# First-layer softmax sums: two more groups of a batch, and six of the first batch, added up by VectorE in place of TensorE

## The chip, the cores and the metric

The kernel runs on one core of a Trainium2 chip. The metric is the device time of one execution in microseconds (us). The engines are TensorE (PE; PEld is its weight load), VectorE (DVE), ScalarE (ACT), GpSimd (POOL) and SyncE (SP), which here only issues DMAs.

## The reference, cut to what matters

Two layers, each a group norm, an attention over 1024 tokens of 512 channels, a projection and a residual, for a batch of 8 images of 32 x 32. All is 32-bit float. The change is in the attention of the first layer (16 heads of 32 channels):

```python
attn = jnp.einsum('bhid,bhjd->bhij', q * SCALE, k)
attn = jax.nn.softmax(attn, axis=-1)
out = jnp.einsum('bhij,bhjd->bhid', attn, v)
```

The second layer has 4 heads of 128 channels and adds relative position logits to its scores. A softmax row's sum is over all 1024 keys j; the kernel keeps keys on partitions, so that a sum over keys is a sum across partitions.

## The kernel before, in words

**Tiling.** Channels or keys lie on the 128 partitions. `attention_0` works in 8 groups per batch: a group is 4 heads (index m, in the order 0, 2, 1, 3; `HB` is 4 heads of `D0` = 32 channels) and a half h of the queries (`NB` = 512). Each group has 8 blocks of 128 keys (`NT`), so a batch has 64 steps. A step's `front` makes the scores of 4 heads on TensorE (L886: 32-row weights, two halves of the keys) into one 4-bank PSUM tile `ps` with a single buffer, and ScalarE's exponential (L901) writes 128 x 2048 numbers into one of three slots of `e_room`. The step after it, `back` multiplies the values with them on TensorE (L912) into the PSUM bank `acc`, which also has one buffer, and VectorE adds the block onto the group's running sum (L924, 7 of 8 blocks), in place in the slot of the group's first block. The slot of an ended group's sums goes back into the turn, and the exponential of the third block of the next group writes it.

**Sums of a group, two ways.** At the first step after a group has ended, a helper divides by the row sums:
- `finish` (L930): TensorE multiplies the 4 running sums with ones (L934), 8 instructions (a 32-bit matmul is two), into the `acc` bank. `normalise` has ScalarE copy them (L764), VectorE transpose (L766), invert (`invert`, L781 and L784) and spread them by another transpose (L796), and GpSimd multiply the group's 128 x 512 output in `q` (L770).
- `sums_apart` (L865) with the class `Apart` (L807): for a list of groups, `take` (L818) has VectorE transpose each head's running sum in blocks of 32 x 32 (L826) and reduce it (L829) into a column of `few_0`. It does two heads in one step and two in the next (the second half only behind the last product add, `reader[0]`). After the last group of the list, `fold_up` (L837) has TensorE add the 32 remaining partials of all its groups at once (L841, 8 short instructions) into a `bank`, VectorE inverts them, and `quotient` (L852), one group a step, spreads (L796) and has GpSimd multiply (L857).

`apart_of(b)` (L138) gives the lists of batch b. Before, `APART` is one list (2, 3, 4); batch 0 has none, batch 1 has (2, 3), batch 7 has (3, 4). In batches 2 to 6 the list (2, 3, 4) is not folded in place: `sums_apart` puts it into `aside`, and it is folded, inverted and multiplied at the end of the second layer's attention, which runs in the middle of the batch.

**Rings of tiles.** Tiles of one tag share buffers in turn, and a new tenant waits until the last one has been read. `rec`, two buffers of 128 x 512, serves `normalise`, `take` and `quotient`. `columns`, two buffers of the same size, holds the column part of the second layer's position logits: `Seeds.load` (L1037) brings one tile per 8 steps of `attention_1` by a DMA on SP, and GpSimd adds it (L1064). `bank`, three PSUM banks, serves the products and the folding.

**What sets the order.** The projections are made in seven products of half size (`seven`, L506): x, y and z are banks, `a` and `b` (L520, L528) are VectorE adds that read a bank between two products into it, and `c12`, `c21` (L682, L685) finish a quarter. `side_by_side` (L1611) interleaves the 64 steps of `attention_0` of batch b with the rest of the work, by costs: the first layer's output projection of b-1 and the second layer's of b-2, the second layer's projections, its attention (cost 0: it runs in one piece, at about step 42 of 64), and the first layer's projections for b+1 (`before_0`). In batch 0 only the rest of its own projections and `before_0` of batch 1 stand beside it, together with the preparation of weights on GpSimd (`other_sums`, L182). `issue_after` keeps an instruction behind another of its engine; apart from that the framework orders each engine's instructions by itself.

In the trace, batch 0's attention runs from 58 to about 306 us, batch 1's from there to 726, and a batch of 2 to 6 takes 442.0 us from one point to the same in the next. The second layer's attention of batch 1 (beside batch 2's first layer) lies from 952 to 1061; groups 5, 6 and 7 of batch 2 end at about 1091, 1131 and 1168.

Of the kernel before, what the change touches and what calls it, by code (L numbers as in the profile page):

```python
# [9 lines left out]
F32 = mybir.dt.float32  # L10
# [7 lines left out]
P = 128  # L18
# [4 lines left out]

BLOCKS = 8

APART = [(2, 3, 4)]


@with_exitstack
def quick_path(  # L30
# [25 lines left out]
    B, IH, IW, C = x.shape  # L56
# [3 lines left out]
    NB = 512  # L60
# [9 lines left out]
    mem = ctx.enter_context(tc.tile_pool(name="mem", bufs=1))  # L70
# [18 lines left out]
    def wide_tile(name, shape=None):  # L89
        return wide[0][1].tile(shape or [P, NB // P, NB], F32, tag="ps", name=name, bufs=1)  # L90
# [47 lines left out]
    def apart_of(b):  # L138
        if b == 1:
            return [(2, 3)] + APART[1:]  # L140
        return [] if b == 0 else [(3, 4)] if b == B - 1 else APART

    n_checks = B * CC * NH + 2 * 4 + B - 2
    n_checks -= sum(len(some) - 1 for b in range(B) for some in apart_of(b))
    checks = consts.tile([P, n_checks], F32, tag="checks", name="checks")
    check_at = [0]
# [10 lines left out]
    class Matrix:  # L157
# [3 lines left out]
        def __init__(self, w, col0, name):  # L161
            self.name = name
            self.w = w.rearrange("(cc p) n -> p cc n", p=P)[:, :, col0 : col0 + NB]
# [60 lines left out]
    class Stream:  # L224
# [43 lines left out]
        def take(self, i):  # L268
            got = self.tiles.pop((self.at, i)) if self.plan[self.at][2] else self.tiles[self.at, i]
            return got  # L270
# [487 lines left out]
    def normalise(dst, acc_sums, name, engine=nc.gpsimd):  # L758

        su = mem.tile([P, NB], F32, tag="rec", name=f"su_{name}", bufs=2)
        nc.scalar.copy(su, acc_sums)  # L764
        turned = mem.tile([P, NB], F32, tag="rec", name=f"tu_{name}", bufs=2)
        nc.vector.transpose(turned, su)  # L766
        few, rec = [turned.rearrange("p (t c) -> p t c", c=32)[:, :, i] for i in range(2)]
        invert(rec, few, few)
        spread(su, rec)
        engine.tensor_tensor(dst, dst, su, op=ALU.mult)  # L770
# [36 lines left out]
    class Apart:  # L807


        def __init__(self, b, some):  # L810
            self.b, self.some = b, some
            self.groups = []
            self.width = len(some) * (NB // 32)

        def place(self, r):
# [2 lines left out]
        def take(self, m, h, esum, dst):  # L818
            at = len(self.groups)
            self.groups.append((m, h, dst))  # L820
            for r0 in range(0, HB, 2):
                turned = []
                for r in (r0, r0 + 1):
                    t = mem.tile([P, NB], F32, tag="rec", name=f"tu_0_{self.b}_{m}_{h}_{r}", bufs=2)
                    with tc.issue_after(reader[0].ins) if r0 else nullcontext():
                        nc.vector.transpose(t, esum[:, r, :])  # L826
                    turned.append(t)
                for r, t in zip((r0, r0 + 1), turned):
                    nc.vector.tensor_reduce(  # L829
                        few_0[:, r, at, :],  # L830
                        t.rearrange("p (t c) -> p t c", c=32),
                        axis=AX.X,
                        op=ALU.add,
                    )
                yield
# [23 lines left out]
    def attention_0(q, k, v, b, blocks=range(NT)):  # L859

        steps = [(m, h, j) for m in (0, 2, 1, 3) for h in range(NH) for j in blocks]
        state = {}
        aparts = {i: part for some in apart_of(b) for part in [Apart(b, some)] for i in some}

        def sums_apart(i, m, h, esum):  # L865
            part = aparts[i]
            together = i == 4 and b < B - 1
            if together:
                aside.append(part)
            yield from part.take(m, h, esum, q[m][:, h * NB : (h + 1) * NB])  # L870
            if together or i != part.some[-1]:
                return
            part.fold_up()
            for i in range(len(part.some)):
                yield
                part.quotient(i)

        def front(m, h, j):
            name = f"0_{b}_{m}_{h}_{j}"
            ps = wide_tile(f"ps_{name}")  # L880
            for i in range(2):

                some = slice(64 * i, 64 * i + 64)
                for r in range(HB):
                    rows = slice(r * D0, (r + 1) * D0)
                    nc.tensor.matmul(  # L886
                        ps[some, r, :],
                        k[m][rows, j * P + 64 * i : j * P + 64 * i + 64],
                        q[m][rows, h * NB : (h + 1) * NB],
                        start=True,  # L890
                        stop=True,
                    )
            at = turn.pop(0)
            if j == blocks[0]:

                turn.append(sum_at[0])
                sum_at[0] = at
            else:
                turn.append(at)
            e = e_room[:, at]  # L900
            exps[0] = nc.scalar.activation(e, ps, AF.Exp, scale=D0 ** -0.5)  # L901
            return e

        def back(m, h, j, e):
            name = f"0_{b}_{m}_{h}_{j}"
            if j == blocks[0]:
                state["acc"] = psum.tile([P, NB], F32, tag="acc", name=f"acc_{name}", bufs=1)
                state["first"] = e
            acc = state["acc"]
            for r in range(HB):  # L910
                c0 = (m * HB + r) * D0
                nc.tensor.matmul(  # L912
                    acc[r * D0 : (r + 1) * D0, :],
                    v[:, j, c0 : c0 + D0],
                    e[:, r, :],
                    start=(j == blocks[0]),
                    stop=(j == blocks[-1]),
                )
            if j == blocks[1]:
                state["esum"] = state["first"]  # L920
            if j != blocks[0]:

                with tc.issue_after(reader[0].ins) if beside_norm[0] else nullcontext():
                    summed[0] = nc.vector.tensor_add(state["esum"], state["esum"], e)  # L924
            if j != blocks[-1]:
                return
            nc.scalar.copy(q[m][:, h * NB : (h + 1) * NB], acc)
            state["ended"] = (m, h, state["esum"])

        def finish(m, h, esum):  # L930
            name = f"0_{b}_{m}_{h}"
            su = psum.tile([P, NB], F32, tag="acc", name=f"sums_{name}", bufs=1)
            for r in range(HB):
                nc.tensor.matmul(  # L934
                    su[r * D0 : (r + 1) * D0, :],
                    ones,
                    esum[:, r, :],
                    start=True,
                    stop=True,
                )  # L940
            normalise(q[m][:, h * NB : (h + 1) * NB], su, name)

        pending = None
        ended, ending = 0, []
        for at in steps:
            if "ended" in state:
                if ended in aparts:
                    ending.append(sums_apart(ended, *state.pop("ended")))
                else:
                    finish(*state.pop("ended"))  # L950
                ended += 1
            for part in ending:
                next(part, None)
            e = front(*at)
            if pending is not None:
                back(*pending)
            pending = (*at, e)
            yield 2
        for part in ending:
            run(part)  # L960
        back(*pending)
        yield 1
        finish(*state.pop("ended"))
# [643 lines left out]
    def run(part):  # L1607
        for _ in part:
            pass
# [671 lines left out]
```

## Time and profile before

| | before |
|---|---|
| median of 3 runs | 3623.51 us (3623.4 to 3626.25) |
| profiled execution: time, span | 3626.2 us, 3624.4 us |
| PE busy | 3604.8 us (99%) |
| DVE busy | 2573.9 us (71%) |
| ACT busy | 1990.6 us (55%) |
| POOL busy | 1399.2 us (39%) |
| granted PE clock | 0.999 |

The profiled execution is one of the program; its span runs from the first to the last instruction, and its time has 1.8 us around that. A line of the groups gives the line of the code, engine, operation, tile written and tiles read, shapes and count, then busy time in all and mean ns of one, and last the idle time just before them with what ended it. A timeline line gives the start and the length in us, then the same, and x is how many instructions are merged. In a line of a window the columns are the window, its length, the busy us of PE, PEld, DVE, ACT and POOL, the clock, the DMA share and GB/s. Ends of matmuls are modelled, so the pace of TensorE is best read from the starts.

### The profile page before, as it was taken

To read this page: it belongs to the slowest core of one execution; us is meant where nothing else is said; L and a number is where in the kernel's file an instruction comes from. 1 tells how busy PE (TensorE), PEld (TensorE's weight loads), DVE (VectorE), ACT (ScalarE), POOL (GpSimd) and SP (SyncE) were. 2 spreads that over 40 slices of the span, in tenths; PEclk is the share of its full clock that TensorE was granted. 3 is DMA by queue.
4 is the path that set the end of the run, shared out by engine and by line. 5 is a ranking of instruction groups with operands and counts; after the bars stand their busy time and mean duration, and the time that the engine had idled before them with its cause. 6 is when DMAs were issued, how large, how long until landed. Compare 5 with 4: busy or idle time off the path is not lost.

```text
span 3624.4 us, 80755 instructions
## 1 busy us (share of the span) xinstructions
PE 3604.8 (99%) x33786; PEld 1230.2 (34%) x33786; DVE 2573.9 (71%) x2807; ACT 1990.6 (55%) x2266; POOL 1399.2 (39%) x880
## 2 busy tenths in 40 slices
PE   9999999999999999999999999999999999999999
PEld 4232244232433234332343323433234232323343
DVE  6788656787667966679666796667966678667546
ACT  3555666446664466544665446654566545656254
POOL 1343055231552316523075230742318312166255
PEclk9999999999999999999999999999999999999999
DMA  6233164242643426344363433624336133324376
GB/s 192 73 111 104 44 175 137 64 145 68 187 126 89 131 66 195 110 112 112 84 195 90 135 97 101 186 74 139 85 101 203 55 101 79 103 91 158 97 200 155
DMA packets 577316, 431.96 MB, mean 119 GB/s; under 512 B 274320, under 2 KB 467632, under 8 KB 575920
## 3 DMA queue, kind: packets, MB, share of 16 engines
q1 hardware_dynamic: 567952, 411.05, 40.7%
q0 software_dynamic: 2608, 13.70, 1.0%
q8 instruction: 268, 4.39, 0.5%
q10 hardware_dynamic: 6384, 1.97, 0.2%
q14 instruction: 104, 0.85, 0.1%
HBM read 334.30 MB, written 92.27 MB: 118 GB/s over the span
## 4 chain that ended last, share of the span: by engine, by line
PE 96%; DVE 2%; ACT 1%; issue 1%; DMA 0%; POOL 0%; SPq 0%; DVEq 0%; ACTq 0%; POOLq 0%
PE ps L886 15%; PE acc L912 14%; PE ps L1139 12%; PE acc L1153 12%; PE y_v L430 5%; PE y_q L430 4%; PE y_k L430 4%; PE z_v L430 3%; PE x_v L430 3%; PE z_q L430 3%; PE x_k L430 3%; PE x_q L430 3%; PE z_k L430 3%; PE y_wp L430 2%; PE y_wo L430 2%; PE x_wp L430 2%
## 5 line engine op out<-in xcount | busy, mean ns | idle before, releaser
L901 ACT ACTIVATE e_room<-ps 128x2048 f32<-128x2048 f32 x512 | 962.0, 1879 | 749.8 <-PE ps L886 728.1
L924 DVE TENSOR_TENSOR e_room<-e_room 128x2048 f32<-128x2048 f32 x448 | 1093.4, 2441 | 375.2 <-ACT e_room L901 373.7
L1064 POOL TENSOR_TENSOR pos<-pos,columns 128x512 f32<-128x512 f32 x448 | 642.8, 1453 | 179.5 <-DMA pos<-pr 178.0
L886 PE MATMUL ps<-q,k 32*64 32x512 f32 x8192 | 594.0, 613 | 2.1 <-ACT e_room L901 2.0
L912 PE MATMUL acc<-e_room,v 128*32 128x512 f32 x4096 | 546.8, 604 | 0.0
L1139 PE MATMUL ps<-q,k 128*128 128x512 f32 x1024 | 527.3, 598 | 0.3 <-ACT ps L1073 0.3
L1153 PE MATMUL acc<-e,v 128*128 128x512 f32 x1024 | 523.9, 594 | 0.0
L1142 ACT ACTIVATE e<-ps 128x512 f32<-128x512 f32 x512 | 305.8, 597 | 316.9 <-PE ps L1139 308.8
L1169 DVE TENSOR_TENSOR es<-es,e 128x512 f32<-128x512 f32 x384 | 276.7, 721 | 285.1 <-ACT e L1142 282.4
L1153 PEld LDWEIGHTS acc<-e,v 128*128 128x128 f32 x1024 | 193.6, 190 | 248.1 <-issue 134.0
L1139 PEld LDWEIGHTS ps<-q,k 128*128 128x128 f32 x1024 | 191.0, 190 | 254.9 <-issue 229.7
L1073 ACT COPY ps<-pos 128x512 f32<-128x512 f32 x448 | 264.8, 592 | 0.4
L886 PEld LDWEIGHTS ps<-q,k 32*64 32x64 f32 x8192 | 123.1, 130 | 394.7 <-issue 201.2
L912 PEld LDWEIGHTS acc<-e_room,v 128*32 128x32 f32 x4096 | 81.4, 108 | 412.6 <-issue 366.2
L689 POOL TENSOR_TENSOR k<-b_k,p_k 128x512 f32<-128x512 f32 x32 | 49.4, 1544 | 426.6 <-ACT p_k L534 415.8
L770 POOL TENSOR_TENSOR q<-q,su 128x512 f32<-128x512 f32 x45 | 70.3, 1563 | 352.0 <-DVE su L796 328.0
L689 POOL TENSOR_TENSOR v<-b_v,p_v 128x512 f32<-128x512 f32 x32 | 51.8, 1620 | 358.6 <-ACT p_v L534 334.0
L689 POOL TENSOR_TENSOR q<-b_q,p_q 128x512 f32<-128x512 f32 x32 | 62.9, 1967 | 273.0 <-ACT p_q L534 258.5
L1110 POOL TENSOR_TENSOR q<-q,su 128x512 f32<-128x512 f32 x48 | 76.8, 1621 | 180.2 <-DVE su L796 180.0
L993 ACT COPY pos<-pp 32x512 f32<-32x512 f32 x128 | 104.9, 820 | 29.2 <-PE pp L984 27.9
L1167 DVE TENSOR_TENSOR es<-e,e 128x512 f32<-128x512 f32 x64 | 64.2, 1003 | 66.6 <-ACT e L1142 66.6
L1064 POOL TENSOR_TENSOR slots<-slots,columns 128x512 f32<-128x512 f32 x64 | 84.0, 1341 | 22.2 <-DMA slots<-pr 22.1
(246 smaller groups left out, 4613.6 us busy)
## 6 DMA issues: line engine op xcount, KB each, us to landing
pos<-pr SPq DMA_DIRECT2D x448, 256.0 KB, 3.5
w_qkv<-ws_qkv SPq DMA_DIRECT2D x168, 128.0 KB, 2.7
x1T<-d SPq DMA_DIRECT2D x32, 512.0 KB, 5.2
d<-x1T SPq DMA_DIRECT2D x32, 512.0 KB, 3.6
pc<-pos SPq DMA_DIRECT2D x32, 512.0 KB, 6.8
pr<-pos SPq DMA_DIRECT2D x32, 512.0 KB, 7.9
columns<-pc SPq DMA_DIRECT2D x64, 256.0 KB, 4.4
x2T<-d SPq DMA_DIRECT2D x32, 512.0 KB, 6.0
```

The source lines that it names most:

```text
L430: ins = nc.tensor.matmul(out[columns, :], weights[:, columns], moving, start=start, stop=stop, skip_group_check=open_sum,)
L689: nc.gpsimd.tensor_tensor(self.dst[1][1], s(b), s(p7), op=ALU.add)
L886: nc.tensor.matmul(ps[some, r, :], k[m][rows, j * P + 64 * i : j * P + 64 * i + 64], q[m][rows, h * NB : (h + 1) * NB], start=True, stop=True,
L901: exps[0] = nc.scalar.activation(e, ps, AF.Exp, scale=D0 ** -0.5)
L912: nc.tensor.matmul(acc[r * D0 : (r + 1) * D0, :], v[:, j, c0 : c0 + D0], e[:, r, :], start=(j == blocks[0]), stop=(j == blocks[-1]),)
L924: summed[0] = nc.vector.tensor_add(state["esum"], state["esum"], e)
L1064: nc.gpsimd.tensor_tensor(self.rows[i], self.rows[i], self.columns[i // NT], op=ALU.add)
L1073: self.copied = nc.scalar.copy(ps, rows)
L1139: scored[0] = nc.tensor.matmul(ps, k[h][:, keys], q[:, h, queries], start=False, stop=True, skip_group_check=True)
L1142: exps[0] = nc.scalar.activation(e, ps, AF.Exp, scale=1.0 / math.sqrt(D1))
L1153: nc.tensor.matmul(acc, v[:, j, h * D1 : (h + 1) * D1], e, start=(j == 0), stop=(j == NT - 1),)
L1169: added[0] = nc.vector.tensor_add(state["esum"], state["esum"], e)
```

## The change

Three places. `APART` gets a second list, (5, 6), so that batches 1 to 6 treat groups 5 and 6 apart too, folded in place; batch 0 gets the lists (0, 1, 2) and (3, 4, 5), also in place; batch 7 stays. For these lists (`some[0] == 5`, or batch 0) the transposed sums go into the `columns` ring; (2, 3), (2, 3, 4) and (3, 4) stay in `rec`. And a list is only put aside if its last group is group 4, where before group 4 as such was asked for, since in batch 0 group 4 is now in the middle of a list. The number of checks of the sums follows from the lists.

```diff
-APART = [(2, 3, 4)]
+APART = [(2, 3, 4), (5, 6)]
...
     def apart_of(b):
         if b == 1:
             return [(2, 3)] + APART[1:]
-        return [] if b == 0 else [(3, 4)] if b == B - 1 else APART
+        if b == 0:
+            return [(0, 1, 2), (3, 4, 5)]
+        return [(3, 4)] if b == B - 1 else APART
...
             self.groups = []
+            self.tag = "columns" if some[0] == 5 or b == 0 else "rec"
             self.width = len(some) * (NB // 32)
...
-                    t = mem.tile([P, NB], F32, tag="rec", name=f"tu_0_{self.b}_{m}_{h}_{r}", bufs=2)
+
+                    t = mem.tile(
+                        [P, NB], F32, tag=self.tag, name=f"tu_0_{self.b}_{m}_{h}_{r}", bufs=2
+                    )
...
-            together = i == 4 and b < B - 1
+            together = i == part.some[-1] == 4 and b < B - 1
```

## The prediction

> **What bounds the kernel.** I read the page's first part, then its chain, then the groups of instructions by form, then timelines of TensorE, VectorE and ScalarE around the places that the change touches.
>
> ```profile
> PE 3604.8 (99%) x33786; PEld 1230.2 (34%) x33786; DVE 2573.9 (71%) x2807; ACT 1990.6 (55%) x2266; POOL 1399.2 (39%) x880
> PE 96%; DVE 2%; ACT 1%; issue 1%; DMA 0%; POOL 0%; SPq 0%; DVEq 0%; ACTq 0%; POOLq 0%
> ```
>
> TensorE has no idle time to win; what shortens the kernel is less work for it, provided that nothing makes it wait afterwards. The groups (busy in all, mean ns of one, then the idle time before):
>
> ```profile
> L924 DVE TENSOR_TENSOR e_room<-e_room 128x2048 f32<-128x2048 f32 x448 | 1093.4, 2441 | 375.2 <-ACT e_room L901 373.7
> L857 POOL TENSOR_TENSOR q<-q,su 128x512 f32<-128x512 f32 x19 | 59.2, 3122 | 20.9 <-DVE su L796 20.9
> L934 PE MATMUL sums<-e_room,ones 128*32 128x512 f32 x360 | 51.2, 596 | 0.4 <-DVE e_room L924 0.4
> L826 DVE STREAM_TRANSPOSE tu<-e_room 128x512 f32<-128x512 f32 x76 | 49.3, 687 | 0.3
> L829 DVE TENSOR_REDUCE few<-tu 128x16 f32<-128x512 f32 x76 | 47.4, 658 | 0.0
> ```
>
> L934 is what goes: 360 instructions are 45 groups of 8. L826 and L829, 76 of each, are the 19 groups that VectorE already adds up, 4 of each per group. What one L934 really costs is the gap between the score matmuls (L886) of neighbouring steps. Timeline of TensorE in batch 2:
>
> ```profile
> 1088.44 1.11 PE L886 MATMUL ps<-q,k 32*64 32x512 f32 x16
> ...
> 1092.09 1.05 PE L934 MATMUL sums<-e_room,ones 128*32 128x512 f32 x8
> 1093.07 1.11 PE L886 MATMUL ps<-q,k 32*64 32x512 f32 x16
> ...
> 1098.55 1.11 PE L886 MATMUL ps<-q,k 32*64 32x512 f32 x16
> ...
> 1102.30 1.11 PE L886 MATMUL ps<-q,k 32*64 32x512 f32 x16
> ```
>
> A step with one product lasts 3.75 us (1098.55 to 1102.30), the one with the sum 4.63 (1088.44 to 1093.07): the sum costs 0.88, not its 1.05. In the first batch's last part it costs more:
>
> ```profile
> 217.41 1.11 PE L886 MATMUL ps<-q,k 32*64 32x512 f32 x16
> ...
> 220.74 1.07 PE L886 MATMUL ps<-q,k 32*64 32x512 f32 x2
> 221.74 1.06 PE L934 MATMUL sums<-e_room,ones 128*32 128x512 f32 x8
> ...
> 226.06 1.11 PE L886 MATMUL ps<-q,k 32*64 32x512 f32 x16
> ```
>
> There the sum splits the scores (x2, then x14): 5.32 us for a step that otherwise takes 3.33, so 1.98. Now VectorE, first in the windows (busy us, by engine, in 28 and 29 us), then in the chain:
>
> ```profile
> 222.00:250.00 28.00, 28.00 (x360) 9.43 (x352) 22.46 (x18) 17.05 (x12) 13.63 (x7) 1.00 0.31 95
> 250.00:279.00 29.00, 28.90 (x362) 9.59 (x360) 24.46 (x19) 17.04 (x12) 14.11 (x8) 1.00 0.41 142
> ```
> ```profile
> 258.31 3.32 DVE e_room L924
> 262.99 3.19 DVE e_room L924
> ```
>
> VectorE is busy 80 and 84% here, and two of its adds already lie in the chain that sets the end: the first batch has the least cover. In batch 2 there is a hole just where the change puts work:
>
> ```profile
> 1090.64 0.68 DVE L520 TENSOR_TENSOR a_q<-y_q,p_q 128x512 f32<-128x512 f32 x1
> 1093.95 0.71 DVE L766 STREAM_TRANSPOSE tu<-su 128x512 f32<-128x512 f32 x1 [2.64 <-ACT su L764]
> ...
> 1099.30 0.68 DVE L528 TENSOR_TENSOR b_q<-y_q,p_q 128x512 f32<-128x512 f32 x1
> ```
>
> **What the Trainium skill says.** "TensorE: Matmul & The Clock Gate", Part 3 (packing small matmuls): 32-column tiles run side by side in the array. The trace agrees: eight L934 instructions of 0.596 us take 1.05 together, so a sum is cheap to begin with. "PSUM — Partial Sum Buffer", Engine vs sequencer instructions: VectorE's queue is strictly first in, first out. So a late transpose delays the adds behind it. "SBUF — State Buffer", SBUF: two separate sides: a VectorE instruction with two SBUF inputs and a GpSimd instruction exclude each other. The trace agrees: L924 takes 2.29 us alone and 3.18 beside GpSimd's multiply at 1095.96; the added one-input transposes and reductions stay at 0.67 to 0.71 and 0.64 to 0.68 everywhere, so I cost them at their means.
>
> **The change, part by part.** Groups on VectorE go from 19 to 37: six in batch 0, two each in batches 1 to 6; batch 7 keeps its two.
>
> (a) Sums off TensorE. Twelve in batches 1 to 6 at 0.88: 10.6 us. Batch 0: four at about 0.95 (155.46 to 160.19 is 4.73 against 3.76; others 0.88) make 3.8, two at 1.98 (the second: 5.31 from 249.38 to 254.69) make 4.0. Sum 18.4. The `acc` bank also loses its second tenant, and ScalarE 18 copies of 0.586 (L764), 10.5 us; ScalarE is busy 55% and waits for TensorE, so 0 gained.
>
> (b) Foldings on TensorE. Eight new ones (two in batch 0, one each in 1 to 6) of 8 instructions of about 0.2 us, 0.24 to 0.29 together. The one that stands between two score matmuls (477.83, batch 1) leaves a gap of 3.83 against 3.77: 0.06. Bounds 0.06 to 0.29; I take 0.08: 0.6 us. Each takes one of the three banks that the products rotate through and holds it until VectorE has inverted it; the one at 477.83 waited until 481.3 for that and TensorE stood nowhere: 0, up to 1 us each if VectorE is late. The added wait is TensorE's, for the last reduction; scores of that step queue behind it. They come one step (over 3 us) after it, so 0.
>
> (c) VectorE. A group adds 4 x 0.687 + 4 x 0.658 = 5.4 us, in halves of 2.7 in two neighbouring steps, and drops a transpose (0.70), an inversion (0.26 + 0.19 + 0.08); its spreading transpose stays. Net 4.2 per group, and about 0.6 to invert a fold: 18 x 4.2 + 8 x 0.6 = 80 us on VectorE, which is idle for 1050. So the sum fits; only places can fail. The order on an engine is not the code's (b_q is emitted ahead of the add at 1096.20 and runs after it), so new work can also reorder old: 0, with 3 us either way in the range.
>
> Group 5 of batches 2 to 6: the sums are complete at 1090.7, so the first half fills the hole from 1091.3 to 1093.95 free of cost. The second is bound behind b_q (1099.30) and pushes what follows. Walking on, all 0.88 earlier: b_q gains 1.3, then the spreads are 1.8 late, the add at 1103.3 1.2, a_k at 1113.96 0.7. TensorE wants a_k by 1115.17 with 0.53 to spare: a stall of 0.2. The exponentials of the group's third block must wait for the last transpose (their tile is the old sums'): 0.7 late, with nearly as much slack: 0.15. Group 6 (1132 to 1144) finds VectorE idle before and after: 0. So 0.4 a batch, bounds 0 and 2.7 (one half wholly in TensorE's way); six batches 2.4.
>
> Batch 0: group 0 fills the hole of 3.1 us before 97.60: 0. Groups 1 to 3 come among forms and transposes; b_q at 152.40 has 0.55 us to spare and about 0.3 to 1 us of lateness reaches it, a_k at 197.99 likewise: 1.2 together. Group 4 has a hole of 2.8 (before 223.56): 0. Group 5: step time is 3.33 and an exponential ends 3.1 after its scores begin, so any late add stops TensorE after 0.2 us. From 250 to 272 VectorE gets 4.2 for group 5, 0.6 for the inversion and two spreads of 0.69 beyond its own share: 6.2. Idle before there: 2.0 + 0.4 + 0.9. The rest, 2.8, and the 2.0 that TensorE would have gained itself, are lost to VectorE: 4.8, bounds 0 and 9 (if GpSimd, which has four subtractions of prep_o from 256.97 to 267.3 in its queue, holds a spread's tile as well). Batch 0 stalls: 6.0.
>
> (d) Tiles. The transposes take the `columns` ring, whose other tenants are DMAs issued on SP and read by GpSimd. GpSimd's last read in that period ends at 1048.8, the first new transpose comes at 1091, the last by 1146; the next columns DMA is issued at 1363. No wait either way, so nothing on SP's queue is held: 0. GpSimd's multiplies by the quotient stay 18 for 18, 1.28 alone and 3.3 where VectorE adds; they come about two or three steps after the folding and nobody waits before the next products: 0.
>
> Sum: 18.4 - 0.6 - 2.4 - 6.0 = 9.4 us less. The profiled execution took 3626.2 (span 3624.4): it would be 3616.8. The median of the runs shown is 2.7 lower: 3623.5 - 9.4 = **3614.1**.
>
> **Rivals.** (1) VectorE's order absorbs it all, as for the 19 groups of before, where TensorE waits for L826 or L829 nowhere: 3623.5 - 17.8 = 3605.7. Against it: most of those lie where VectorE is busy 57 to 65% (windows 1336 to 1382 and 1297 to 1336). (2) VectorE sets the pace in the whole of batch 0 and keeps 1 us a batch more: 18.4 - 0.6 - 11 - 6 is 0.8 less, 3622.7. For it: the two adds in the chain. (3) Slower: the second half, 2.7 us, lands ahead of the product add (L520, L528) or the exponential that TensorE waits for, at every group. 18 x 2.7 = 49 less 17.8 gives 31 more: 3654. It decides the sign from 1.0 us per group (17.8 / 18). Against it: the existing halves stand behind such adds, and holes lie beside most of the new ones. (4) That the sums stay on TensorE cannot be: their count follows from the lists.
>
> **Chances.** Forecast (3609.5 to 3617) 0.50; rival 1 (3604 to 3609.5) 0.22; rival 2 (3617 to 3628) 0.18; rival 3 0.10. The range 3605 to 3622 holds the forecast, nearly all of 1 and half of 2: 0.8. About 0.2% (7.2 us, below 3616.3) is what a measurement of this kernel can tell from no change. Faster by more: 0.22 + nine tenths of 0.50 = 0.67; slower by more 0.12; between 0.21.
>
> **What would show it.** After: L934 x216, L826 and L829 x148, L841 with 8 foldings more; steps with a take as long as their neighbours in batches 1 to 6; TensorE's waits for VectorE, or steps over 3.4 us, between 250 and 275. If batch periods (442.0 before) shrink by less than 1 us, (c) is wrong in the steady part; if batch 0 ends 7 us earlier, it is wrong there; if a `columns` DMA waits for VectorE, (d) is.

## The result, and the profile after

| | before | after |
|---|---|---|
| median | 3623.69 us (3623.4 to 3626.25) | 3646.22 us (3641.96 to 3650.31) |
| ratio of the times | 1 | 1.0061, 95% interval 1.0047 to 1.0076 |
| profiled execution: time, span | 3626.2, 3624.4 us | 3641.96, 3640.1 us |

The change makes the kernel 22.5 us slower, where 9.4 us less was forecast. Lines of the code are 2 to 6 higher now: the scores are L892, the exponential L907, the values' product L918, VectorE's adds L930, the sums by ones L940; the transposes of a take are L832, its reductions L835, the folding L847, the spreads L798. First part and chain of the page after:

```profile
PE 3594.6 (99%) x33706; PEld 1229.6 (34%) x33706; DVE 2626.7 (72%) x2903; ACT 1980.5 (54%) x2248; POOL 1393.1 (38%) x880
PE 93%; DVE 4%; ACT 1%; issue 1%; POOL 1%; DMA 0%; SPq 0%; ACTq 0%; DVEq 0%; POOLq 0%
```

TensorE has 10.2 us less to do than before (3604.8), yet the span is 15.7 longer. So the time is in idle stretches (45.5 us of the span, 19.6 before); a lower clock in places also makes the same work count as busy for longer. VectorE's part of the chain went from 2 to 4%. The groups (busy, mean ns, idle before):

```profile
L930 DVE TENSOR_TENSOR e_room<-e_room 128x2048 f32<-128x2048 f32 x448 | 1080.3, 2411 | 391.6 <-ACT e_room L907 389.6
...
L832 DVE STREAM_TRANSPOSE tu<-e_room 128x512 f32<-128x512 f32 x148 | 97.1, 686 | 0.6
L835 DVE TENSOR_REDUCE few<-tu 128x16 f32<-128x512 f32 x148 | 91.9, 658 | 0.0
...
L940 PE MATMUL sums<-e_room,ones 128*32 128x512 f32 x216 | 31.4, 596 | 1.2 <-DVE e_room L930 1.2
L847 PE MATMUL sums<-few,fold 128*32 128x48 f32 x56 | 3.1, 216 | 6.9 <-DVE few L835 6.9
L847 PE MATMUL sums<-few,fold 128*32 128x32 f32 x64 | 2.2, 195 | 0.3 <-DVE few L835 0.3
```

The counts are those forecast (L940 x216, L832 and L835 x148), and their durations too. New is the last column of the foldings: 6.9 us of TensorE's idle time lie ahead of them. TensorE's waits (total, times, longest):

```profile
PE ps L892 <- ACT e_room L907: 17.9, 13, 2.9
PE sums L847 <- DVE few L835: 7.2, 4, 3.5
```

The first of these rows was 2.0 us in the profile of before, and the second was not in it. I laid the start of each of the 512 exponentials beside that of before, step by step. A step that lost its sum brings the next exponential forward by 0.86 to 0.93 us, one in batch 0 by 1.98. The losses are steps too: with its gains counted, batch 0 leaves the kernel 6.9 us late in the first steps of batch 1, and each of batches 2 to 6 jumps by 3.58 us in the third block after group 5 (0.54 comes back a block later where the clock holds, so 3.04 is the bare shift).

**Group 5 of batch 2.** VectorE, ScalarE and TensorE there (start, length, what, idle before):

```profile
1101.78 2.29 DVE L930 TENSOR_TENSOR e_room<-e_room 128x2048 f32<-128x2048 f32 x1 [1.53 <-ACT e_room L907]
1103.98 0.68 DVE L530 TENSOR_TENSOR b_q<-y_q,p_q 128x512 f32<-128x512 f32 x1
1104.59 1.29 DVE L798 STREAM_TRANSPOSE su<-few 128x512 f32<-128x512 f32 x2
1105.80 0.67 DVE L832 STREAM_TRANSPOSE tu<-e_room 128x512 f32<-128x512 f32 x1
1107.52 0.71 DVE L798 STREAM_TRANSPOSE su<-few 128x512 f32<-128x512 f32 x1 [1.05 <-POOL q L1116]
1108.16 0.67 DVE L832 STREAM_TRANSPOSE tu<-e_room 128x512 f32<-128x512 f32 x1
...
1108.92 1.88 ACT L907 ACTIVATE e_room<-ps 128x2048 f32<-128x2048 f32 x1 [4.03 <-DVE tu L832]
...
1110.85 1.12 PE L892 MATMUL ps<-q,k 32*64 32x512 f32 x16 [2.91 <-ACT e_room L907]
```

The second half of the take may not start before b_q (`issue_after`). After b_q the framework put two spreads of the second attention's quotients, then one transpose, then a third spread, of the list put aside. This one waits 1.05 us for a tile of `rec` that GpSimd still reads, and only then comes the last transpose. It reads the slot that the third block's exponential is to write, so ScalarE stands 4.03 us, the exponential comes 3.58 us later in its step than before, and TensorE, which has one `ps` tile, stands 2.91 us.

**The first folding.** TensorE and VectorE in batch 0:

```profile
155.11 1.07 PE L918 MATMUL acc<-e_room,v 128*32 128x512 f32 x8
159.64 0.27 PE L847 MATMUL sums<-few,fold 128*32 128x48 f32 x2 [3.47 <-DVE few L835]
...
161.98 2.01 PE L892 MATMUL ps<-q,k 32*64 32x512 f32 x16
...
151.64 6.04 DVE L930 TENSOR_TENSOR e_room<-e_room 128x2048 f32<-128x2048 f32 x2
157.72 1.30 DVE L832 STREAM_TRANSPOSE tu<-e_room 128x512 f32<-128x512 f32 x2
158.95 1.24 DVE L835 TENSOR_REDUCE few<-tu 128x16 f32<-128x512 f32 x2
```

The folding stands in TensorE's queue ahead of the next scores, while VectorE is behind: its two adds took 6.04 us beside GpSimd. So TensorE stands 3.47 us, and the scores after it take 2.01 instead of 1.11 us, since the clock is lower there. Windows of the profile after (length, busy us of PE, PEld, DVE, ACT and POOL, clock, DMA share, GB/s), each from the end of such a wait:

```profile
159.60:164.80 5.20, 4.83 (x36) 0.98 (x39) 3.55 (x6) 0.70 (x1) 1.37 (x2) 0.67 0.58 227
1554.20:1563.00 8.80, 8.80 (x96) 2.33 (x96) 7.17 (x7) 4.35 (x3) 2.03 (x2) 1.00 0.11 32
1997.50:2006.00 8.50, 8.48 (x56) 1.83 (x56) 6.74 (x6) 1.88 (x1) 0.17 (x1) 0.63 0.05 15
2443.90:2453.00 9.10, 9.10 (x84) 2.12 (x88) 6.94 (x6) 3.26 (x3) 1.65 (x2) 0.81 0.11 31
```

The same wait of 2.91 us is followed by a lower clock in batches 4 and 5 and not in batch 3.

**Theories.** A, mine: places in queues. The second half of group 5's take stands behind b_q and mixed with spreads that wait for GpSimd, and batch 0's foldings stand too early in TensorE's queue. B: VectorE's extra load as such, wherever it stands. C: the clock is the main loss. A third rival came from the prediction: the second half in TensorE's way at every group.

### The profile page after: what moved, and what is told of

Read it like the earlier page. It is cut to its first block, busy times and chain, and to the rows that moved or that the text cites. A ratio compares the mean times of both kernels' runs of the same rounds, so it can differ in the third digit from the quotient of the medians.

```text
span 3640.1 us, 80688 instructions
## 1 busy us (share of the span) xinstructions
PE 3594.6 (99%) x33706; PEld 1229.6 (34%) x33706; DVE 2626.7 (72%) x2903; ACT 1980.5 (54%) x2248; POOL 1393.1 (38%) x880
## 4 chain that ended last, share of the span: by engine, by line
PE 93%; DVE 4%; ACT 1%; issue 1%; POOL 1%; DMA 0%; SPq 0%; ACTq 0%; DVEq 0%; POOLq 0%
PE ps L892 14%; PE acc L918 13%; PE ps L1145 12%; PE acc L1159 12%; PE y_v L432 4%; PE y_k L432 4%; PE y_q L432 4%; PE x_v L432 3%; PE z_q L432 3%; PE x_k L432 3%; PE z_v L432 3%; PE x_q L432 3%; PE z_k L432 3%; PE y_wp L432 2%; PE y_wo L432 2%; DVE e_room L930 2%
## 5 line engine op out<-in xcount | busy, mean ns | idle before, releaser
L907 ACT ACTIVATE e_room<-ps 128x2048 f32<-128x2048 f32 x512 | 962.2, 1879 | 790.9 <-PE ps L892 739.6
L930 DVE TENSOR_TENSOR e_room<-e_room 128x2048 f32<-128x2048 f32 x448 | 1080.3, 2411 | 391.6 <-ACT e_room L907 389.6
L892 PE MATMUL ps<-q,k 32*64 32x512 f32 x8192 | 593.0, 615 | 17.9 <-ACT e_room L907 17.9
L918 PE MATMUL acc<-e_room,v 128*32 128x512 f32 x4096 | 548.1, 606 | 0.0
L892 PEld LDWEIGHTS ps<-q,k 32*64 32x64 f32 x8192 | 122.8, 130 | 404.1 <-issue 190.1
L918 PEld LDWEIGHTS acc<-e_room,v 128*32 128x32 f32 x4096 | 81.4, 108 | 414.6 <-issue 374.0
L1116 POOL TENSOR_TENSOR q<-q,su 128x512 f32<-128x512 f32 x48 | 64.5, 1364 | 204.2 <-DVE su L798 204.2
L772 POOL TENSOR_TENSOR q<-q,su 128x512 f32<-128x512 f32 x27 | 46.2, 1711 | 235.8 <-DVE su L798 224.8
L863 POOL TENSOR_TENSOR q<-q,su 128x512 f32<-128x512 f32 x37 | 89.8, 2437 | 38.9 <-DVE su L798 38.9
```

The costliest lines, as they stand in the source:

```text
L892: nc.tensor.matmul(ps[some, r, :], k[m][rows, j * P + 64 * i : j * P + 64 * i + 64], q[m][rows, h * NB : (h + 1) * NB], start=True, stop=True,
L918: nc.tensor.matmul(acc[r * D0 : (r + 1) * D0, :], v[:, j, c0 : c0 + D0], e[:, r, :], start=(j == blocks[0]), stop=(j == blocks[-1]),)
```

## The experiments

Each was timed beside the kernel before (3623.6 to 3623.9 us there).

**Batch 0 as before (e1_steady).**

```diff
-            return [(0, 1, 2), (3, 4, 5)]
+            return []
```

> Groups 5 and 6 of batches 1 to 6 by VectorE, batch 0 as before the change. Theory A (places in the queues): twelve gains of 0.86 us and the fold's loss of 1.3 us in batch 1, but five times 3.05 us of TensorE's wait for the third block's scores tile in batches 2 to 6, and 0 to 8 us of half-speed clock behind these waits: 6 to 14 us slower than before, about 3632 us; the profile shows five waits of some 2.9 us at the scores' line for the exponential, in the second block after each batch's group 5. Theory B (VectorE's extra load as such): two thirds of the 22 us, as twelve of the eighteen added groups are here: 3638 us, spread over many small waits. Theory C (the clock): the waits cost little by themselves, and the loss is where the granted clock is under 0.9.

Measured 3638.38 us, ratio 1.004 (1.0026 to 1.0054): 14.8 us slower. All five waits of 2.91 us are there. In the profile the bare shift is 3.04 us each, 15.2 in all; half clock behind four of the five adds 7.9 us, batch 1 loses 1.3 and the twelve sums gain 10.3. The time is just past A's upper end (14 us), and it is B's own figure too; the five waits in place of many small ones speak for A.

**Batch 0 alone (e2_first).**

```diff
-APART = [(2, 3, 4), (5, 6)]
+APART = [(2, 3, 4)]
```

> Only batch 0's six groups by VectorE, batches 1 to 7 as before the change. Theory A: gains of 6.3 us (five of 0.86 and one of 1.99) against some 13 us of losses in batch 0, of which the two foldings, which stand in TensorE's queue directly ahead of the next scores and wait there for VectorE's last reductions, take 8: about 7 us slower than before, 3631 us, with the waits of some 3.5 us and 3.1 us at the first and the second folding. Theory B (load as such): one third of 22 us, 3631 us too, but without two big waits. Theory C (the clock): no loss but where the clock drops.

Measured 3634.12 us, ratio 1.0029 (1.0018 to 1.004): 10.6 us slower, with waits of 3.5 and 2.8 us at the two foldings. Both theories gave 3631 us, so only the two waits tell them apart. The two parts make 25.4 us, against 22.5 together: they are about additive.

**The second half unbound (e3_unbound).**

```diff
-                    with tc.issue_after(reader[0].ins) if r0 else nullcontext():
+                    with tc.issue_after(reader[0].ins) if r0 and self.some[0] != 5 else nullcontext():
```

> The changed kernel with one thing undone: the second half of group 5's and group 6's transpositions isn't bound behind the normalisation's b_q any more, so that it stands directly behind the first half on VectorE. The work of VectorE is the same. Theory A: the third block's exponential no longer waits for the second half behind the spreads, so the five waits of 2.9 us and what clock they lose go: 18 to 24 us below the changed kernel, about 3624 us. Theory B (load as such): nothing changes, 3646 us. The third rival of the prediction (the second half ahead of what the normalisation waits for costs 2.7 us a group): the five waits are replaced by others at the exponential or the product, and the time stays at 3640 us or over.

Measured 3623.31 us, ratio 0.9998 (0.999 to 1.0007): 22.9 us below the changed kernel with the same work and, matmul for matmul, the same order on TensorE. The same place in this kernel, VectorE and then ScalarE:

```profile
1099.21 1.29 DVE L832 STREAM_TRANSPOSE tu<-e_room 128x512 f32<-128x512 f32 x2
1100.43 1.24 DVE L835 TENSOR_REDUCE few<-tu 128x16 f32<-128x512 f32 x2
1101.59 2.28 DVE L930 TENSOR_TENSOR e_room<-e_room 128x2048 f32<-128x2048 f32 x1
1103.79 0.68 DVE L530 TENSOR_TENSOR b_q<-y_q,p_q 128x512 f32<-128x512 f32 x1
1104.38 1.29 DVE L798 STREAM_TRANSPOSE su<-few 128x512 f32<-128x512 f32 x2
...
1104.39 1.89 ACT L907 ACTIVATE e_room<-ps 128x2048 f32<-128x2048 f32 x1 [0.44 <-PE ps L892]
```

The last transpose is over at 1100.5, in time that VectorE had idle (1.53 us ahead of the add in the kernel after). b_q is no later for it, and the exponential now waits for its scores. Each of batches 2 to 6 is 1.67 us shorter than before, nearly the 1.73 of its two sums. B falls for these batches, and so does the third rival: the half is harmful behind b_q, not ahead of it. Batch 1's loss, which I had put down to its folding, went from 1.28 to 0.40 us. There group 6's second half stood behind b_k with no spread ahead of it, and the third block's exponential waited for it all the same. So the guard alone, without the spreads, cost 0.9 us at that place; whether it would be harmless at group 5 with the transposes directly behind b_q was not tested.

**Foldings behind later scores (e4_fold_later).**

```diff
-            part.fold_up()
+            part.fold_up(True)
...
-        def fold_up(self):
+        def fold_up(self, here=False):
...
-                ins = nc.tensor.matmul(
+                with tc.issue_after(scores_0[0].ins) if here else nullcontext():
+                    ins = nc.tensor.matmul(
```

Here `scores_0[0]` is the score matmul emitted last.

> The changed kernel with one thing moved: foldings inside the loop of blocks are bound behind the scores emitted last, so they stand one or two blocks later in TensorE's queue. The work is the same. Theory A: TensorE's waits for VectorE's reductions at the first and second folding of batch 0 (3.5 and 3.1 us, with the clock behind the first) and batch 1's (1.3 us) go: 9 us below the changed kernel, about 3637 us. Theory B (load as such): nothing changes, 3646 us. Theory C (the clock): 2 us less where the first folding's half clock goes.

Measured 3638.29 us, ratio 1.004 (1.0026 to 1.0053): 7.9 us less, though the two kernels' intervals overlap. The waits at the foldings are gone. But TensorE now waits 2.6 us for a_q and 3.3 us for exponentials in batch 0, and from step to step it came only 3.1 us earlier into batch 1 than in e3_unbound. Batch 1 still loses its 1.28 us, so that was not the folding. Hence a fourth theory, B2: VectorE is full in batch 0, so that a wait taken away comes back elsewhere. The window of group 2's steps, in the kernel before and then after:

```profile
126.00:158.00 32.00, 31.62 (x333) 7.79 (x334) 28.67 (x20) 17.84 (x15) 23.15 (x13) 1.00 0.36 120
```
```profile
126.00:158.00 32.00, 30.18 (x314) 7.07 (x314) 31.76 (x23) 17.75 (x14) 25.26 (x12) 1.00 0.38 121
```

VectorE's busy time goes from 28.67 to 31.76 of 32 us.

**Unbound, and batch 0 as before (e8_unbound_steady).** The edits of e1 and e3 together.

> Groups 5 and 6 of batches 1 to 6 by VectorE with the second half unbound, batch 0 as before the change. Unbinding took the five waits and batch 1's too away, and the profile of that run still lost 6.9 us by the start of batch 1. Both theories: this loss goes, 3623.3 less 6.9 is 3616.5 us, 7 us faster than before; anything over 3620 would say that the two parts of the change hinder each other.

Measured 3614.88 us, ratio 0.9973 (0.9963 to 0.9984). That is 8.9 us faster than the kernel before: the twelve sums of batches 1 to 6 are worth nearly what they cost on TensorE (twelve times 0.86 is 10.3).

**Both edits (e5_both).** Those of e3 and e4.

> Second half unbound and foldings in the loop of blocks moved behind later scores. Theory A as first put (the place of the folding is what costs in batch 0): 3623.3 less some 9, 3614 us. Theory B2 (VectorE is full in batch 0, 31.8 of 32 us in its group 2, so a wait that is taken away comes back at the next thing TensorE needs from VectorE): only 3 us, as the start of batch 1 came only 3.1 us earlier when the foldings alone were moved: 3620 us.

Measured 3619.25 us, ratio 0.9987 (0.998 to 0.9993): 4.1 us below e3_unbound, as B2 has it, and not the 9 of A.

**Only groups that fall where VectorE has slack (e9_slack).** In batch 0 the list is (0, 2, 4), folded in place.

> Second half unbound, and in batch 0 only groups 0, 2 and 4 by VectorE, as one list folded after group 4: their transpositions fall in groups 1, 3 and 5, where VectorE was busy 22 of 32, 25 of 32 and 18 of 24 us before the change, and not in group 2, where it was busy 29 of 32. Theory B2 (VectorE's slack): gains of 0.86, 0.86 and 1.99 with little loss: 3.7 us under the kernel with batch 0 as before, 3613 us. Theory A as first put (the folding's place): a wait of about 3 us at the one folding, so 3616 us. Theory B (load as such): half of batch 0's loss of 13 less the gain of 3.7, so 3619 us.

Measured 3620.18 us, ratio 0.9989 (0.9982 to 0.9995): 5.3 us above e8_unbound_steady, worse than every expectation. TensorE waited 2.1 us at the folding, 2.1 for exponentials and 1.2 for b_k. So the mean slack of a group does not say whether a take is free there.

**The load without its use (e10_load).** On top of e8:

```diff
+                    if b == 0 and ended < 6:
+                        part = loads.setdefault(ended // 3, Apart(0, (0, 1, 2)))
+                        ending.append(part.take(*state["ended"], None))
                     finish(*state.pop("ended"))
```

> Second half unbound; in batch 0 the transpositions and reductions of groups 0 to 5 are made by VectorE at the same places, but nothing uses them: TensorE still makes these groups' sums, and there are no foldings in batch 0. So it is VectorE's load alone, without gain and without the foldings' waits. Theory A as first put: no loss against the kernel with batch 0 as before, 3616 us. Theory B2: TensorE waits elsewhere in batch 0 for VectorE's other work, 5 to 8 us: 3622 to 3625 us.

Measured 3617.49 us, ratio 0.9982 (0.9974 to 0.999): 2.6 us above e8, half or less of what B2 wanted (5 to 8 us), though VectorE is as busy between the fourth step of batch 0 and the sixth of batch 1 as with both edits (236.1 and 234.6 us). TensorE's idle time in that stretch is 1.8 us here and 8.3 with both edits. So it seems that what comes with the folding (the inversion, three spreads, three multiplies of GpSimd) costs more than the takes. This is not clean, as TensorE still makes its sums here, and so gives VectorE more time in these steps. The place in e5_both, VectorE and then TensorE:

```profile
170.35 0.70 DVE L799 STREAM_TRANSPOSE su<-few 128x512 f32<-128x512 f32 x1
171.61 0.71 DVE L799 STREAM_TRANSPOSE su<-few 128x512 f32<-128x512 f32 x1 [0.56 <-POOL q L865]
172.24 6.00 DVE L932 TENSOR_TENSOR e_room<-e_room 128x2048 f32<-128x2048 f32 x2
178.17 0.68 DVE L523 TENSOR_TENSOR a_q<-y_q,p_q 128x512 f32<-128x512 f32 x1
...
178.90 1.05 PE L433 MATMUL y_q<-f_xn,w_qkv 128*32 128x512 f32 x2 [2.62 <-DVE a_q L523]
```

a_q stands behind two adds of 3.00 us each instead of 2.25, while GpSimd multiplies from 168.33 to 176.09, and these behind the spreads.

**Spreads further apart (e12_spaced, e13_forced).** On top of both edits; the second binds too:

```diff
             for i in range(len(part.some)):
                 yield
+                if b == 0:
+                    yield
-                part.quotient(i)
+                part.quotient(i, summed[0] if b == 0 else None)
```

> Both edits (second half unbound, foldings behind later scores), and in batch 0 each of a list's three spreads comes one step later still than the one before it, so two steps apart instead of one. If in batch 0 the bunch of take, inversion and three spreads, with GpSimd's three multiplies that slow VectorE's adds, is what makes a_q 2.6 us late, this wait goes or halves: 3616 to 3617.5 us. If VectorE has too much in batch 0 wherever it stands, the wait only moves: 3619 us, as before this edit.

Measured 3618.33 us, ratio 0.9985 (0.9978 to 0.9992), not to be told from both edits alone. The first list's spreads stood at the same times as before (170.36, 171.62), as the framework orders VectorE by itself, and a_q is as late: there the edit did not do what it said. (Of the second list one spread did move, from 262.65 to 281.69, and a wait of 1.15 us for an exponential behind it went.) So I bound them:

> As the kernel with spaced spreads, whose spreads the scheduler left where they had been on VectorE; now each of the first batch's spreads is also bound behind the last add, so that they do come two steps apart and a_q of batch 1 stands behind one add fewer. If the bunch of spreads, and the adds that GpSimd's multiplies slow behind it, is what TensorE waits for in batch 0, its 2.6 us for a_q goes or falls under 1 us: 1.5 to 3 us less than with both edits alone, 3616 to 3618 us. If VectorE has too much to do in batch 0 wherever it stands, the wait comes back at another place: 3619 us.

Measured 3614.87 us, ratio 0.9977 (0.9968 to 0.9986): 4.4 us less than both edits, and below the 3616 to 3618 expected. VectorE in this kernel:

```profile
167.84 4.68 DVE L934 TENSOR_TENSOR e_room<-e_room 128x2048 f32<-128x2048 f32 x2
172.44 0.70 DVE L799 STREAM_TRANSPOSE su<-few 128x512 f32<-128x512 f32 x1
173.07 2.25 DVE L934 TENSOR_TENSOR e_room<-e_room 128x2048 f32<-128x2048 f32 x1
175.24 0.68 DVE L523 TENSOR_TENSOR a_q<-y_q,p_q 128x512 f32<-128x512 f32 x1
```

One spread instead of three stands ahead of a_q, the adds take 2.3 us, a_q comes 2.9 us earlier and TensorE no longer waits for it. So here too place decided.

**The tiles (e11_spread_ring, e7_rec).** On the changed kernel, every second spread tile in another ring; and the takes back in `rec`:

```diff
-            su = mem.tile([P, NB], F32, tag="rec", name=f"su_1_{b}_{h}_{c}", bufs=2)
+            su = mem.tile([P, NB], F32, tag=("rec", "es1")[i % 2], name=f"su_1_{b}_{h}_{c}", bufs=2)
```
```diff
-            self.tag = "columns" if some[0] == 5 or b == 0 else "rec"
+            self.tag = "rec"
```

> The changed kernel, with every second of the second attention's spread tiles in another ring of the same size, so that the third spread that stands between the two transpositions of group 5's second half no longer waits for GpSimd's multiply (1.05 us in batch 2). The second half is still bound behind b_q and the first two spreads. If the wait for GpSimd is what makes the third block's exponential late, it ends 1 us earlier in each of batches 2 to 6: TensorE's five waits fall from 2.9 to about 1.9 us, 5 to 6 us below the changed kernel, and more if the clock then holds: 3636 to 3641 us. If the places in the queue alone count, the waits stay at 2.9 us: 3646 us.

Measured 3644.15 us, ratio 1.005 (1.0037 to 1.0064); so the 3636 to 3641 expected did not come, and against the changed kernel it is unclear. The five waits fell from 2.91 to 2.26 us: the third spread waited 0.40 us for GpSimd instead of 1.05, and those 0.65 us came through whole, though here both transposes stand behind all three spreads. Most of the wait is thus the order, not GpSimd.

> The changed kernel with the transposed tiles of all lists in the ring of two that the spreads use, as the lists of before do; the logits' ring is left as it was. If the ring of tiles matters, group 5's last transposition has to wait for a further multiply of GpSimd, 1.3 to 3.3 us: the five waits of TensorE grow from 2.9 to 4 to 6 us, 3652 to 3662 us. If it doesn't (the prediction's step on the tiles), nothing changes: 3646 us.

Measured 3664.32 us, ratio 1.011 (1.0094 to 1.0125): 18 us worse than the changed kernel. Its VectorE, then TensorE's waits:

```profile
1112.67 0.71 DVE L798 STREAM_TRANSPOSE su<-few 128x512 f32<-128x512 f32 x1 [1.64 <-POOL q L1116]
1113.89 0.71 DVE L832 STREAM_TRANSPOSE tu<-e_room 128x512 f32<-128x512 f32 x1 [0.51 <-POOL q L1116]
1115.12 0.71 DVE L832 STREAM_TRANSPOSE tu<-e_room 128x512 f32<-128x512 f32 x1 [0.51 <-POOL q L863]
```
```profile
PE ps L892 <- ACT e_room L907: 30.3, 14, 4.8
```

Each tile of the take now waits for one more multiply, and batch 1 has a new wait of 3.29 us. The ring of the change is its good part.

## Why the prediction was wrong

- **(a) Sums off TensorE, 18.4 us.** Right at the sums' own steps: twelve times 0.86 in batches 1 to 6, and in batch 0 0.86 three times, 0.97 once and 1.99 twice, 7.5 us where 7.8 was forecast. The step of group 4's sum, 5.32 us before, is as long as its neighbours now:

```profile
222.06 1.11 PE L892 MATMUL ps<-q,k 32*64 32x512 f32 x16
...
225.38 1.11 PE L892 MATMUL ps<-q,k 32*64 32x512 f32 x16
```

What the forecast's sum of terms left out is the order of TensorE's other work. Batch 0's 64 steps and the first three of batch 1, in e8_unbound_steady and then in e13_forced:

```profile
58.02:305.24 247.22, 246.84 (x2855) 70.79 (x2853) 201.66 (x184) 140.97 (x103) 90.05 (x48) 1.00 0.35 102
305.24:319.33 14.09, 14.09 (x126) 3.27 (x125) 10.67 (x12) 7.40 (x6) 3.25 (x2) 1.00 0.09 25
```
```profile
58.29:300.91 242.62, 239.38 (x2795) 69.22 (x2793) 221.60 (x213) 137.12 (x96) 92.51 (x47) 1.00 0.36 103
300.91:318.67 17.76, 16.82 (x157) 3.98 (x153) 13.70 (x13) 7.93 (x7) 4.46 (x3) 1.00 0.15 40
```

TensorE is busy 7.5 us less in batch 0, but 2.7 more in the three steps after it, where 28 matmuls of the output projection stand that ran in batch 0 otherwise. The same 2.7 to 2.8 us are in e5_both and e9_slack and not in e10_load, whose TensorE keeps the old order. The forecast had "new work can also reorder old" only as a band of 3 us. Why the framework orders it so was not tested.
- **(b) Foldings.** 0.6 us on TensorE was about right. "They come one step (over 3 us) after it, so 0" failed: in batch 0 VectorE was a step late itself, and the folding's place ahead of the scores turned that into 3.47 and 3.08 us. The trace of before had no folding where VectorE was 90% busy; around its seven it was busy 56 to 76%.
- **(c) Group 5 of batches 2 to 6, 0.4 us each, is the step that decided the sign.** Its mechanism was named, the third block's exponential waiting for the last transpose, but "0.7 late" was 3.58. I had let the transposes follow b_q directly and pushed the spreads behind them; the framework put three spreads ahead of the last one, one with a wait for GpSimd that the trace of before showed in the same place (1.48 us). The note that new work can reorder old was costed at "0, with 3 us either way in the range", as one mishap, where it comes at the same place in five batches: 15.2 us where 2.0 was forecast, and the clock on top, which the forecast left out. Group 6 at 0 was right in batches 2 to 6; batch 1 lost 1.3 us there.
- **(c) Batch 0, 6.0 us.** The stalls are some 10 us (from its fourth step to batch 1's sixth TensorE is busy 251.3 of 261.7 us; it was idle 0.5 before), at the foldings, a_k, b_v and the sums' line, mostly not at group 5's late adds.
- **(d) Tiles.** Right: TensorE waits for no `columns` transfer, and e7_rec shows the ring to be worth 18 us.
- **The rivals.** The third was nearest, with the exponential as its price and the right sign, but it wanted 2.7 us at all 18 groups; it was 3.0 at five, and the rest of the loss had other places. The second, VectorE setting the pace of batch 0, was half right: the stalls there are real, but they follow the order (e13_forced). That e8 and e13 reach the forecast's own time (3614.9 us) is chance, as neither is the kernel that it was made for.
- **Theory C** is a part, not the cause: unbinding removes the idle time and the clock's losses with it. How the 22.9 us of e3_unbound divide between the two in the median runs stays open; between the two profiled runs (20.3 us apart) they are about 15 and 4.7, with 0.9 in batch 1, and the profiled run after is the fastest of its four.
- **What is left.** With every edit, batch 0's sums gain nothing in the medians (e13 equals e8). Between its fourth step and batch 1's sixth TensorE is busy 4.7 us less than in e8 (249.8 and 254.5) and idle 3.8 more (4.2 and 0.4), in waits of up to 0.9 us. The load alone cost 2.6 us in e10, at other places. Whether another order gets these gains was not tried.

## What to carry to other kernels

When work is moved to an engine that feeds the bottleneck, its idle total says little; list what will stand ahead of the last instruction on which the bottleneck depends, with the waits of those neighbours, and multiply by the number of times the place recurs. A guard that keeps new work behind an urgent instruction can put it into a worse spot: freeing it turned 22.5 us of loss into none, and with batch 0 left alone into 8.9 us of gain. A short instruction on the bottleneck that needs a slow engine's result belongs behind work that doesn't, as its queue waits with it; here that was worth 4.1 us of the 9 hoped for, as the next late result was close behind. And after a change of the work, look at what else the bottleneck's own queue does in another order: here 2.7 us of a gain of 7.5 went there.

## What the runs showed of the hardware

In these traces the length of an idle stretch doesn't alone decide TensorE's clock after it. In four kernels with the five waits (after, e1, e4, e11) the clock over the 9 us after a wait of 2.26 to 2.91 us was 0.65 to 0.81 in 13 of 20 cases and 1.00 in 7; after the five of 4.76 us in e7_rec it was 0.67 to 0.76 each time. The Trainium skill, "TensorE: Matmul & The Clock Gate", Why this matters for your kernels, asks for no gaps over some 3 us between bursts of matmuls; here shorter ones were followed by a lower clock too. After 2.26 us it came in four of five cases in e11, at 1.6 us each. A wait of 1.04 us in batch 7, which every kernel here has, was followed by 0.62 in three of the fourteen profiles, one of them that of before: its batch 7 is 3.0 us longer than that of the profile after.

The slower runs of the changed kernel had the lower mean clock (3650.31 us at 0.995, 3641.96 at 0.998), so such drops fit its spread of 8 us. They needn't be behind the five waits: e13_forced, without these, spreads by 6.0 us, and e8_unbound_steady by 2.2.
